# The two score products of a pair of batches put directly behind the attends of the pair before, in the steady step lists of a graph attention kernel

## The chip, the cores and the metric

The kernel runs on one core of one Trainium2 chip. Its time is the device time of one execution in microseconds (us). A run with a profile gives besides that a record of every instruction. Below, PE is TensorE's matmuls and PEld its weight loads, DVE is VectorE, ACT is ScalarE, POOL is GpSimd and SP is SyncE, whose only work here is to issue DMAs.

## The reference

There are 128 batches of 128 nodes with 512 features, and one 128 x 128 adjacency matrix for each batch. Two layers follow one another, each with a residual and a layer norm; all of it is float32.

```python
x: (128, 128, 512) f32;  adj: (128, 128, 128) int32

# layer 0: attention with 8 heads of 64 features
q, k, v = (x @ W + b for W, b in ((Wq, bq), (Wk, bk), (Wv, bv)))
logits = einsum('bqhd,bkhd->bhqk', q, k) / sqrt(64)
attn = softmax(where(adj > 0, logits, -1e9), axis=-1)
out = relu(einsum('bhqk,bkhd->bqhd', attn, v) @ Wo + bo)
x = layernorm(x + out)

# layer 1: one head with additive scores
Wh = x @ W
e = leaky(s_i + s_j)           # s: Wh times the two halves of the vector a
att = softmax(where(adj > 0, e, -1e9), over one node axis)
x = layernorm(x + leaky(att @ Wh))
```

## The kernel before

**Products.** The large products are done by schemes of seven half-size products in place of eight (the names p1 to p7). The products with Wq, Wk and Wv run over groups of four batches (`GROUP`), in six chains a group: Q, K and V, each in two rounds (`group_product`, L658, matmul L681). Their results go to three PSUM banks (`ps_st`, tiles st_y, st_w, st_x) and are taken out by ScalarE copies (L694) and VectorE additions (L715); six, four, three, four, three and four additions a chain then combine them (`combine`, L731). The weights beyond those that stay in SBUF come in through a ring of four buffers w_n (`fetch_until`, L623). The products with Wo and with layer 1's W run over pairs of batches (`pair_product`, L793, matmul L801), in the classes `LayerZero` (z) and `LayerOne` (w).

**Softmax.** `Softmax` (L855) is layer 0's attention of one batch. Its methods are, in order: `scores` (L868; sixteen matmuls L875 on 64-row tiles, two PSUM banks lg), `add` of the mask (L889, twice), `reduce` (maxima, L898), `exp` (ScalarE, L909, eight heads), `reciprocals` (L919), `divide` (ScalarE, L923), `store` of the probabilities to DRAM (L930), `fetch` of them in another layout (L936, four DMAs into the single buffer paz), `transpose` (VectorE, L942), `attend` (sixteen matmuls L955 on 64-column tiles, one bank p_oT) and `copy` (four on ScalarE, L970). The trip through DRAM and back does one half of turning the probabilities, the VectorE transpose of 32 x 32 blocks the other.

**Layer 1.** `Edge` (L1157) is the attention of layer 1 for one batch: `turn_blocks` (L1187), `add` (L1191), `maxima` (L1197), `exp` (L1201), `divide` (L1205 and L1206), `product` (L1211, bank p_h), `copy` (ScalarE, L1218, into the single `z_slot`), `residual` (L1221), `stats` (L1003 and L1005), `rstd` (GpSimd, L1009 and L1011), `apply` (L1024) and `store` (out_dram). `Senders` (v) writes and fetches the node scores ez (L1262).

**PSUM.** `psum` (L201) gives out five banks in turn to p_h, p_oT, lg and the pair products; the group products have their own three.

**Order.** The schedule is written by hand (`tc.manual_schedule`, L1276): every engine executes its instructions in the order in which the Python code issues them. The steady loop (L1541) makes one step for each batch t from 6 to 123, 118 steps, and issues the tokens of the list `STEADY[t % 4]` (L72 to L114) one after the other. In an even step, f is the softmax of batch t and s that of batch t + 1, and both go on through the odd step behind it, at whose end they attend. The letters are:

- f and s the softmaxes; w and z the pair products of layer 1 and 0; e the layer 1 attention, n the end of the batch before's; v the senders; g and p the end of layer 0 (sums, norm, stores, transposes of x1); m the loads, turns and masks of batches to come (x_pair and x_one load x through SP, sum sums x on GpSimd);
- `h` half of the next group product's step on TensorE;
- `a` and `d` the next copy (ACT) or addition (DVE) left over from these;
- `k` and `k.v` the next combination (L731) on GpSimd or VectorE;
- `i.s1a` and the like a part of the inner sums of x (L500) on GpSimd, with `.v` on VectorE;
- `q` the next fetches of weights w_n, through SP.

Of the kernel before, what the change touches and what calls it, by code (L numbers as in the profile page):

```python
# [70 lines left out]

STEADY = {  # L72
    0: """
        k.v n.residual q f.scores h h m.masks m.sum.0 m.sum.1 m.sum.2 m.sum.3 k.v g.apply.0
        q k.v w.p1 f.add.0 f.add.1 g.store.0 e.turn_blocks a e.add m.cast w.t0 s.scores
        f.reduce w.p6 f.exp.0.1 f.exp.2.3 d w.t2 f.exp.4.5 f.exp.6.7 d n.stats s.add.0
        f.reciprocals.0 s.add.1 e.maxima f.reciprocals.1 s.reduce w.p5 h n.rstd w.p7 w.p2 h
        h m.residuals q g.fetch_both a w.t3 e.exp q q w.c22 w.c11 f.divide.2.3 s.exp.2
        f.divide.0.1 a f.divide.6.7 e.divide w.p4 w.p3 h h h w.c21 s.exp.5 v.senders
        f.divide.4.5 s.exp.0.1 a i.s1a.v n.apply d s.exp.6.7 s.exp.3.4 q n.store v.store  # L80
        f.store g.transpose.1 g.transpose.0 i.s3a.v e.product h m.x_pair i.s2a i.s1b m.turn
        d k.v m.mask i.s3b.v a s.reciprocals.0 s.reciprocals.1 w.c12 d i.s2b.v k.v e.copy
        v.fetch
    """,
    1: """
        p.sum.0 z.by n.residual h z.p2 h k h a s.divide.5.6 i.s4a a f.fetch z.p1 h h d
        n.stats n.rstd k.v m.turn e.turn_blocks s.divide.3.4 s.divide.7 s.divide.0.1
        s.divide.2 n.apply z.bw z.t0 h z.p6 z.t2 a m.cast z.p5 z.p7 k k k h z.c11
        f.transpose z.t3 e.add d z.p4 s.store z.c22 a z.p3 h h m.mask e.maxima z.c21 s.fetch
        n.store q e.exp a a d z.stats.1 e.divide i.s4b h e.product h f.attend z.c12 e.copy  # L90
        f.copy p.sum.1 z.rstd.1 p.sum.2 z.apply.1 s.transpose q z.stats.0 d s.attend s.copy
        p.sum.3 z.rstd.0 k k s.sum.2 s.sum.0 s.sum.1 k s.sum.3 m.x_one z.store.1
    """,
    2: """
        f.scores n.residual g.apply.0 w.p1 f.add.1 f.add.0 s.scores e.turn_blocks w.t0 e.add
        w.p6 f.reduce w.t2 w.p2 h w.p7 m.turn k.v k.v f.exp.4.5 f.exp.6.7 f.exp.0.1 k.v w.p5
        h w.t3 a f.exp.2.3 n.stats f.reciprocals.1 w.c22 e.maxima w.c11 f.reciprocals.0
        e.exp f.divide.2.3 n.rstd w.p4 h w.c21 v.senders a d n.apply f.divide.4.5
        f.divide.6.7 f.divide.0.1 e.divide s.add.0 s.add.1 d h w.p3 q g.store.0 m.residuals
        m.masks h e.product h h a a g.fetch_both m.x_one n.store v.store s.reduce  # L100
        g.transpose.0 w.c12 q f.store v.fetch q m.cast d g.transpose.1 m.mask s.exp.5 e.copy
    """,
    3: """
        s.exp.3.4 z.by s.exp.6.7 k.v n.residual n.stats p.sum.0 h f.fetch a s.exp.2 z.p2
        z.p1 h h s.exp.0.1 z.t0 n.rstd q k.v z.p6 p.sum.1 p.sum.2 s.reciprocals.0
        s.reciprocals.1 d s.divide.5.6 a s.divide.0.1 s.divide.7 s.divide.3.4 h
        e.turn_blocks n.apply d z.t2 s.divide.2 m.cast m.turn h a a h z.p7 h h d m.mask
        z.c11 z.bw e.add a z.t3 k k k e.maxima f.transpose k z.p5 q e.exp h h z.p4 h a a d
        z.c22 s.store q q e.divide z.c21 s.fetch z.p3 h d z.stats.1 z.c12 k h n.store
        e.product z.rstd.1 p.sum.3 z.apply.1 d z.stats.0 h h f.attend s.transpose a e.copy a  # L110
        s.attend f.copy s.copy k z.rstd.0 s.sum.0 q z.store.1 s.sum.2 s.sum.1 m.x_one
        s.sum.3
    """,
}  # L114

# [1607 lines left out]
```

## Time and profile before

| | |
|---|---|
| median of 3 runs | 2329.5 us (2326.45 to 2329.78) |
| the profiled execution | 2328.13 us, span from first to last instruction 2325.5 us |
| granted TensorE clock | 0.993 of full |
| DMA, mean over the span | 233 GB/s |
| HBM read and written | 388.96 and 148.31 MB |

Of the groups of instructions those that the lists move most are these: line, engine, operation, tiles written and read, count, then busy time in us and mean ns of one, then idle time of the engine just before them and what ended it.

```profile
L875 PE MATMUL lg<-out_K,out_Q 64*128 64x128 f32 x2048 | 148.7, 285 | 0.8 <-DVE out_K L731 0.8
L955 PE MATMUL p_oT<-pa,out_V 128*64 128x128 f32 x2000 | 136.7, 279 | 18.7 <-DVE pa L942 18.7
L942 DVE STREAM_TRANSPOSE pa<-paz 128x1024 f32<-128x1024 f32 x125 | 154.6, 1237 | 9.6 <-DMA paz<-pa_dram 7.7
L1009 POOL TENSOR_SCALAR ve<-mv 128x1 f32<-128x1 f32 x256 | 77.9, 304 | 288.6 <-DVE mv L1005 226.3
```

The matmuls of one engine overlap, so a mean of 285 ns is the time from start to modelled end of one, not the distance of two. The forms 64*128 and 128*64 after MATMUL are the part of the array that is used: rows by columns.

### The profile page before, as it was taken

How to read it: one execution, taken by the hardware profiler on the slowest of the kernel's cores; microseconds unless marked ns; L12 is line 12 of the kernel's file. 1: busy time of each engine (PE TensorE's matmuls, PEld its weight loads, DVE VectorE, ACT ScalarE, POOL GpSimd, SP SyncE). 2: the span in 40 equal slices, each digit the busy share in tenths (PEclk: the TensorE clock that was granted, in tenths of full speed). 3: DMA queues.
4: the chain of work that ended last, by engine and by line, in shares of the span. 5: the costliest groups of instructions: out<-in, count | busy, mean ns of one | idle time of the engine just before them, and what ended most of it. 6: DMA issues, size and time to landing. Idle time of an engine off the chain costs nothing.

```text
span 2325.5 us, 53031 instructions
## 1 busy us (share of the span) xinstructions
PE 2264.5 (97%) x17394; PEld 2028.0 (87%) x17394; DVE 2116.6 (91%) x4248; ACT 1665.8 (72%) x5971; POOL 1465.7 (63%) x1735
## 2 busy tenths in 40 slices
PE   5999999999999999999999999999999999999998
PEld 5888988888988888889889889889888889888885
DVE  7998999999999999999999999999999999999977
ACT  1766776777777867767767767767767777777686
POOL 4466666667666666666676666676656666666656
PEclk7999999999999999999999999999999999999999
DMA  6978888888888888878888888888888888888774
GB/s 160 269 209 234 238 249 233 233 232 243 242 241 238 230 236 243 242 240 236 225 246 233 250 238 231 233 240 236 247 238 232 234 244 236 243 238 227 221 217 145
DMA packets 516595, 540.81 MB, mean 233 GB/s; under 512 B 100568, under 2 KB 394336, under 8 KB 516320
## 3 DMA queue, kind: packets, MB, share of 16 engines
q1 hardware_dynamic: 516000, 537.17, 80.8%
q8 instruction: 138, 2.26, 0.4%
q14 instruction: 137, 1.12, 0.2%
q10 hardware_dynamic: 320, 0.26, 0.0%
HBM read 388.96 MB, written 148.31 MB: 231 GB/s over the span
## 4 chain that ended last, share of the span: by engine, by line
PE 58%; DVE 19%; DMA 8%; POOL 5%; SPq 4%; issue 3%; ACT 3%; DVEq 0%; POOLq 0%; ACTq 0%
PE p_y L801 14%; PE st_y L681 14%; PE p_w L801 6%; PE lg L875 6%; PE st_w L681 6%; PE st_x L681 5%; DMA w_n<-wv 4%; DVE pa L942 4%; PE p_x L801 4%; PE p_oT L955 3%; DVE arena L1047 2%; DVE cells L715 2%; PE p_h L1211 2%; DVE st L1003 2%; DMA paz<-pa_dram 2%
## 5 line engine op out<-in xcount | busy, mean ns | idle before, releaser
L909 ACT ACTIVATE pa<-pa,nmax 128x128 f32<-128x128 f32 x1000 | 391.7, 398 | 1.9 <-DVE nmax L898 1.8
L923 ACT ACTIVATE pa<-pa,rs 128x128 f32<-128x128 f32 x1000 | 329.0, 398 | 15.4 <-DVE rs L919 15.2
L1009 POOL TENSOR_SCALAR ve<-mv 128x1 f32<-128x1 f32 x256 | 77.9, 304 | 288.6 <-DVE mv L1005 226.3
L694 ACT COPY cells<-st_y 128x384 f32<-128x384 f32 x288 | 136.2, 473 | 115.8 <-PE st_y L681 102.9
L1024 DVE TENSOR_SCALAR arena<-arena,mv,rstd 128x512 f32<-128x512 f32 x239 | 185.5, 776 | 14.3 <-POOL rstd L1011 14.3
L909 ACT ACTIVATION_READ_ACCUMULATOR pa<-pa,nmax 128x1 f32 x1000 | 194.9, 195 | 0.0
L970 ACT ACTIVATE arena<-p_oT,b_cols 128x128 f32<-128x128 f32 x504 | 144.2, 370 | 64.5 <-PE p_oT L955 60.5
L523 POOL TENSOR_TENSOR x1S<-x1T 128x256 f32<-128x256 f32 x62 | 57.6, 928 | 208.2 <-DVE mf L853 208.2
L1011 POOL TENSOR_TENSOR rstd<-ve,mhalf 128x1 f32<-128x1 f32 x256 | 160.6, 627 | 21.4
L1003 DVE BATCH_NORM_STATS2 st<-arena 128x6 f32<-128x512 f32 x248 | 168.0, 677 | 1.1
L942 DVE STREAM_TRANSPOSE pa<-paz 128x1024 f32<-128x1024 f32 x125 | 154.6, 1237 | 9.6 <-DMA paz<-pa_dram 7.7
L889 DVE TENSOR_TENSOR pa<-lg,mf 128x512 f32<-128x512 f32 x250 | 161.2, 675 | 0.9 <-PE lg L875 0.9
L955 PE MATMUL p_oT<-pa,out_V 128*64 128x128 f32 x2000 | 136.7, 279 | 18.7 <-DVE pa L942 18.7
L694 ACT COPY out_V<-st_y 128x512 f32<-128x512 f32 x128 | 74.5, 582 | 109.5 <-PE st_y L681 109.0
L875 PEld LDWEIGHTS lg<-out_K,out_Q 64*128 64x128 f32 x2048 | 124.2, 187 | 31.9 <-issue 20.4
L875 PE MATMUL lg<-out_K,out_Q 64*128 64x128 f32 x2048 | 148.7, 285 | 0.8 <-DVE out_K L731 0.8
L898 DVE TENSOR_REDUCE nmax<-pa 128x8 f32<-128x1024 f32 x125 | 148.4, 1187 | 0.1
L955 PEld LDWEIGHTS p_oT<-pa,out_V 128*64 128x64 f32 x2000 | 106.7, 136 | 42.0 <-DVE pa L942 33.7
L801 PE MATMUL p_y<-wo_w,x1S 128*128 128x257 f32 x496 | 134.3, 393 | 0.1
L1218 ACT ACTIVATE arena<-p_h 128x512 f32<-128x512 f32 x120 | 71.5, 596 | 87.1 <-DMA out_dram<-arena 59.3
L715 DVE TENSOR_TENSOR cells<-st_w,cells 128x384 f32<-128x384 f32 (+1 forms) x224 | 126.7, 566 | 6.5 <-PE st_w L681 2.9
L801 PE MATMUL p_y<-wo_w,x1T 128*128 128x257 f32 x496 | 131.6, 387 | 0.4 <-ACT arena L812 0.4
(296 smaller groups left out, 7960.2 us busy)
## 6 DMA issues: line engine op xcount, KB each, us to landing
paz<-pa_dram SPq DMA_DIRECT2D x504, 128.0 KB, 3.5
pa_dram<-pa SPq DMA_DIRECT2D x125, 512.0 KB, 3.8
w_n<-wk SPq DMA_DIRECT2D x93, 512.0 KB, 5.9
w_n<-wv SPq DMA_DIRECT2D x93, 512.0 KB, 5.0
w_n<-wk SPq DMA_DIRECT2D x93, 384.0 KB, 4.3
w_n<-wv SPq DMA_DIRECT2D x93, 384.0 KB, 5.6
x_dram<-arena SPq DMA_DIRECT2D x128, 256.0 KB, 2.8
xz<-x_dram SPq DMA_DIRECT2D x240, 128.0 KB, 4.2
```

What stands on the lines that cost most here:

```text
L681: nc.tensor.matmul(p[:, index, :], lhs, rhs, start=start and index == 0, stop=True, skip_group_check=True,)
L694: nc.scalar.copy(dst, p)
L715: nc.vector.tensor_add(cells(c)(h, o), p, t)
L801: nc.tensor.matmul(p[:, :width], xs()[n][:, kc, :], w[:, PLACE[n], kc, :], start=start and kc == 0, stop=True, skip_group_check=True,)
L875: nc.tensor.matmul(self.lg[r][:, c, :], q[rows, 2 * (b % 2) + c % 2, c // 2, :], k[rows, 2 * (b % 2) + c % 2, c // 2, :], start=c == 0, st ...
L889: nc.vector.tensor_add(by_head[:, r * NC : (r + 1) * NC], self.lg[r].rearrange("p c (b k) -> p c b k", b=4), mf.unsqueeze(1).to_broadcast( ...
L909: nc.scalar.activation(self.pa[:, :, h, :], self.pa[:, :, h, :], AF.Exp, bias=self.nmax[:, h : h + 1], accum_out=self.sums[:, h : h + 1],)
L923: nc.scalar.activation(self.pa[:, :, h, :], self.pa[:, :, h, :], AF.Copy, scale=self.rs[:, h : h + 1])
L942: nc.vector.transpose(self.paT.rearrange("p h (a i) -> p a h i", i=32), self.paz.rearrange("p a (h k) -> p a h k", k=32),)
L955: nc.tensor.matmul(self.oT[r * HD : (r + 1) * HD, c, :], v[:, c % 2, c // 2, r * HD : (r + 1) * HD], self.paT[:, r * NC + c, :], start=c == 0,
L1003: nc.vector.bn_stats(st, self.src)
L1024: nc.vector.tensor_scalar(self.src, self.src, self.mv[:, 0:1], self.r, ALU.subtract, ALU.mult)
```

## The change

Only the four step lists are changed; no method and no buffer is. Each list is rearranged:

- `s.scores` stands next to `f.scores` in steps 0 and 2, ahead of `w.p1`. Steps 1 and 3 end with `f.attend` and `s.attend` as before, so TensorE has two attends and two score products in a row.
- `f.fetch` goes from step 1 to the end of step 0.
- Of the inner sums, s1b, s3a, s2a and s4b are on VectorE, in place of s1a, s3a, s3b and s2b. In step 0, `i.s1a` on GpSimd stands ahead of `n.rstd`.
- One combination of a group goes from VectorE (`k.v`) to GpSimd (`k`).
- The group product has 9, 11, 9 and 13 half steps (`h`) in the four steps, where it had 9, 11, 7 and 15. Two heads of `s.exp`, one `k.v` and one `d` go from step 3 to step 2.
- In step 1 `z.apply.1` and `m.mask` stand behind `s.transpose`, in place of ahead of it.

```diff
--- before.py
+++ after.py
@@ -71,45 +71,45 @@
 
 STEADY = {
     0: """
-        k.v n.residual q f.scores h h m.masks m.sum.0 m.sum.1 m.sum.2 m.sum.3 k.v g.apply.0
-        q k.v w.p1 f.add.0 f.add.1 g.store.0 e.turn_blocks a e.add m.cast w.t0 s.scores
-        f.reduce w.p6 f.exp.0.1 f.exp.2.3 d w.t2 f.exp.4.5 f.exp.6.7 d n.stats s.add.0
-        f.reciprocals.0 s.add.1 e.maxima f.reciprocals.1 s.reduce w.p5 h n.rstd w.p7 w.p2 h
-        h m.residuals q g.fetch_both a w.t3 e.exp q q w.c22 w.c11 f.divide.2.3 s.exp.2
-        f.divide.0.1 a f.divide.6.7 e.divide w.p4 w.p3 h h h w.c21 s.exp.5 v.senders
-        f.divide.4.5 s.exp.0.1 a i.s1a.v n.apply d s.exp.6.7 s.exp.3.4 q n.store v.store
-        f.store g.transpose.1 g.transpose.0 i.s3a.v e.product h m.x_pair i.s2a i.s1b m.turn
-        d k.v m.mask i.s3b.v a s.reciprocals.0 s.reciprocals.1 w.c12 d i.s2b.v k.v e.copy
-        v.fetch
+        e.turn_blocks f.scores q m.masks q n.residual k.v g.apply.0 g.store.0 q m.residuals
+        q g.fetch_both q q f.add.0 f.add.1 f.reduce s.scores w.p1 m.sum.0 m.sum.2 m.sum.1
+        e.add m.cast w.t0 h w.p6 h h w.p2 f.exp.2.3 f.exp.4.5 w.t2 f.exp.6.7 a s.add.0
+        m.sum.3 e.maxima d s.add.1 d f.reciprocals.1 n.stats f.exp.0.1 a f.divide.4.5
+        f.reciprocals.0 w.p7 i.s1a h h w.c11 s.reduce d w.p5 w.t3 e.exp f.divide.2.3
+        f.divide.6.7 a f.divide.0.1 s.exp.5 e.divide w.c22 w.p4 h w.p3 n.rstd h n.apply
+        w.c21 v.senders s.exp.2 s.exp.3.4 i.s1b.v i.s3a.v a n.store h g.transpose.1
+        g.transpose.0 e.product s.exp.6.7 s.exp.0.1 v.store f.store h m.x_pair v.fetch
+        f.fetch a e.copy d w.c12 k.v m.mask i.s2b i.s3b i.s2a.v s.reciprocals.0 m.turn
+        s.reciprocals.1 d k
     """,
     1: """
-        p.sum.0 z.by n.residual h z.p2 h k h a s.divide.5.6 i.s4a a f.fetch z.p1 h h d
-        n.stats n.rstd k.v m.turn e.turn_blocks s.divide.3.4 s.divide.7 s.divide.0.1
-        s.divide.2 n.apply z.bw z.t0 h z.p6 z.t2 a m.cast z.p5 z.p7 k k k h z.c11
-        f.transpose z.t3 e.add d z.p4 s.store z.c22 a z.p3 h h m.mask e.maxima z.c21 s.fetch
-        n.store q e.exp a a d z.stats.1 e.divide i.s4b h e.product h f.attend z.c12 e.copy
-        f.copy p.sum.1 z.rstd.1 p.sum.2 z.apply.1 s.transpose q z.stats.0 d s.attend s.copy
-        p.sum.3 z.rstd.0 k k s.sum.2 s.sum.0 s.sum.1 k s.sum.3 m.x_one z.store.1
+        z.p2 n.residual i.s4b.v k.v z.by h h s.divide.7 s.divide.5.6 a a i.s4a s.divide.3.4
+        s.divide.0.1 s.divide.2 z.bw h z.p1 h h z.p5 d n.stats k.v k.v z.t0 z.p6 z.t2 a h
+        z.c11 m.turn e.turn_blocks z.p7 h e.add z.t3 z.p4 f.transpose d n.rstd k p.sum.0 k
+        e.maxima z.c22 s.store a h h q z.p3 s.fetch d n.apply z.c21 a m.cast e.exp a
+        e.divide h h e.product m.x_one n.store q f.attend z.stats.1 p.sum.2 z.rstd.1 p.sum.1
+        z.c12 s.transpose s.attend f.copy z.stats.0 m.mask p.sum.3 e.copy s.copy z.rstd.0
+        s.sum.0 d z.apply.1 s.sum.2 s.sum.1 s.sum.3 k k k z.store.1
     """,
     2: """
-        f.scores n.residual g.apply.0 w.p1 f.add.1 f.add.0 s.scores e.turn_blocks w.t0 e.add
-        w.p6 f.reduce w.t2 w.p2 h w.p7 m.turn k.v k.v f.exp.4.5 f.exp.6.7 f.exp.0.1 k.v w.p5
-        h w.t3 a f.exp.2.3 n.stats f.reciprocals.1 w.c22 e.maxima w.c11 f.reciprocals.0
-        e.exp f.divide.2.3 n.rstd w.p4 h w.c21 v.senders a d n.apply f.divide.4.5
-        f.divide.6.7 f.divide.0.1 e.divide s.add.0 s.add.1 d h w.p3 q g.store.0 m.residuals
-        m.masks h e.product h h a a g.fetch_both m.x_one n.store v.store s.reduce
-        g.transpose.0 w.c12 q f.store v.fetch q m.cast d g.transpose.1 m.mask s.exp.5 e.copy
+        f.scores g.apply.0 q m.masks s.scores w.p1 f.add.0 f.add.1 w.t0 f.reduce h h w.p6
+        f.exp.4.5 f.exp.2.3 w.p2 w.t2 w.p7 e.turn_blocks g.store.0 n.residual s.add.0 k.v
+        k.v k.v f.exp.6.7 e.add w.p5 a s.add.1 m.turn f.reciprocals.1 e.maxima n.stats w.t3
+        f.exp.0.1 f.divide.4.5 h w.p4 a e.exp d h h w.c21 m.cast f.reciprocals.0 w.c11
+        v.senders m.residuals n.rstd n.apply d f.divide.2.3 a a f.divide.6.7 f.divide.0.1 h
+        e.divide m.mask e.product s.reduce d w.c22 k.v h h g.fetch_both m.x_one w.p3 n.store
+        v.store q h f.store q s.exp.6.7 g.transpose.0 v.fetch e.copy s.exp.5 d g.transpose.1
+        w.c12
     """,
     3: """
-        s.exp.3.4 z.by s.exp.6.7 k.v n.residual n.stats p.sum.0 h f.fetch a s.exp.2 z.p2
-        z.p1 h h s.exp.0.1 z.t0 n.rstd q k.v z.p6 p.sum.1 p.sum.2 s.reciprocals.0
-        s.reciprocals.1 d s.divide.5.6 a s.divide.0.1 s.divide.7 s.divide.3.4 h
-        e.turn_blocks n.apply d z.t2 s.divide.2 m.cast m.turn h a a h z.p7 h h d m.mask
-        z.c11 z.bw e.add a z.t3 k k k e.maxima f.transpose k z.p5 q e.exp h h z.p4 h a a d
-        z.c22 s.store q q e.divide z.c21 s.fetch z.p3 h d z.stats.1 z.c12 k h n.store
-        e.product z.rstd.1 p.sum.3 z.apply.1 d z.stats.0 h h f.attend s.transpose a e.copy a
-        s.attend f.copy s.copy k z.rstd.0 s.sum.0 q z.store.1 s.sum.2 s.sum.1 m.x_one
-        s.sum.3
+        a s.exp.3.4 z.by h z.p1 s.exp.0.1 s.exp.2 k k a z.t0 s.reciprocals.1 s.reciprocals.0
+        n.residual d k z.p2 n.stats p.sum.0 h s.divide.5.6 s.divide.3.4 s.divide.2 m.turn
+        e.turn_blocks z.p6 h h m.cast s.divide.7 s.divide.0.1 z.t2 e.add z.bw a a p.sum.1
+        n.rstd p.sum.2 z.p7 z.p5 h h q m.x_one f.fetch z.t3 a q s.store d m.mask n.apply
+        z.c11 e.maxima k p.sum.3 k k z.c22 f.transpose q q z.p4 h h z.p3 h e.exp a z.c21 d
+        z.stats.1 d s.fetch h h z.c12 e.divide n.store e.product a a h h z.rstd.1 z.apply.1
+        d k k k.v z.stats.0 e.copy s.transpose f.attend z.rstd.0 s.attend a f.copy s.copy
+        s.sum.2 s.sum.0 s.sum.1 s.sum.3 z.store.1 q
     """,
 }
```

## The prediction

> **What bounds the kernel now.** I read the page first, then one window over the steady loop, the waits in it, and the TensorE and VectorE timelines of one group of four steps. The page:
>
> ```profile
> span 2325.5 us, 53031 instructions
> PE 2264.5 (97%) x17394; PEld 2028.0 (87%) x17394; DVE 2116.6 (91%) x4248; ACT 1665.8 (72%) x5971; POOL 1465.7 (63%) x1735
> ```
>
> TensorE is busy 97% of the span, VectorE 91%. The window 300 to 2150 us leaves the opening and the ending out:
>
> ```profile
> core 0: us, PE busy (x) PEld busy (x) DVE busy (x) ACT busy (x) POOL busy (x), PEclk, DMA share, GB/s
> 300.00:2150.00 1850.00, 1838.48 (x14222) 1653.20 (x14220) 1706.08 (x3445) 1358.27 (x4901) 1180.12 (x1391) 1.00 0.83 238
> ```
>
> TensorE's gaps are 11.5 us of 1850, at full clock: it is the bound, and only TensorE's time can be won. In the timeline the same product recurs every 70.42 us (1035.17 is followed by its like one group later), so a group of four steps costs 70.42. Per group VectorE has 1706.08 x 70.42 / 1850 = 64.9 us of work, so 5.5 us free. It is nearly a second bound. The waits of the window (engine, line, what for: us in total, times, longest):
>
> ```profile
> ACT arena L1218 <- DMA out_dram<-arena: 52.3, 26, 3.0
> PEld p_oT L955 <- DVE pa L942: 24.1, 52, 0.5
> PEld lg L875 <- issue: 17.6, 78, 0.3
> PE p_oT L955 <- DVE pa L942: 11.5, 52, 0.2
> ```
>
> 52 waits in 26 groups: at every pair of batches the second attend waits for VectorE's transpose L942. Busy TensorE also hides something, seen in start times (start, duration, instruction):
>
> ```profile
> 1035.17 1.09 PE L955 MATMUL p_oT<-pa,out_V 128*64 128x128 f32 x16
> 1036.46 1.09 PE L955 MATMUL p_oT<-pa,out_V 128*64 128x128 f32 x16 [0.20 <-DVE pa L942]
> 1037.49 1.16 PE L875 MATMUL lg<-out_K,out_Q 64*128 64x128 f32 x16
> 1038.58 0.49 PE L681 MATMUL st_x<-w_n,xT 128*128 128x128 f32 x2
> ...
> 1040.47 1.03 PE L801 MATMUL p_y<-wo_w,x1T 128*128 128x257 f32 x4
> 1041.43 1.16 PE L875 MATMUL lg<-out_K,out_Q 64*128 64x128 f32 x16
> 1042.53 1.14 PE L801 MATMUL p_y<-wo_w,x1S 128*128 128x257 f32 x4
> 1043.50 1.03 PE L801 MATMUL p_w<-wo_w,x1S 128*128 128x257 f32 x4
> 1044.37 0.38 PE L681 MATMUL st_y<-w_n,xT 128*128 128x128 f32 x2
> ```
>
> A p_w product of four, 1043.50 to the next start, takes 0.87. The p_y ahead of the lone scores (64-row tiles, L875) takes 0.96 (1040.47 to 1041.43), and the one behind them 0.97 (1042.53 to 1043.50). The 16 scores take 1.10 instead of 0.90, by the records' 112 ns between starts of small matmuls. Thus an island of half-array products between full-array ones costs 0.09 + 0.20 + 0.10 = 0.39 us. Attend, attend and the first scores stand together already, so per pair there are two groups of half-array products: that run and the lone s.scores.
>
> **What the Trainium skill says.** "TensorEngine Tiling (Array Packing)", Key Properties: "Changing tiling mode (not just tile) drains the TensorE". The trace agrees as far as the 0.39 goes; the direct step from attends (128x64 tiles) to scores (64x128) is in both kernels once per pair, so it doesn't enter. "TensorE: Matmul & The Clock Gate", the architectural detail on sub-arrays: VectorE and ScalarE queues are strictly first in, first out, TensorE pulls only weight loads ahead; so a list order is binding, and a late VectorE operation delays all behind it. "SBUF — State Buffer", Who interferes with whom: VectorE operations with a two-port mode and GpSimd share one port pair, exclusively. The trace agrees: L1024 takes 0.54 alone and 0.95 beside GpSimd work:
>
> ```profile
> 1048.99 0.54 DVE L1024 TENSOR_SCALAR arena<-arena,mv,rstd 128x512 f32<-128x512 f32 x1
> 1062.44 1.25 DVE L942 STREAM_TRANSPOSE pa<-paz 128x1024 f32<-128x1024 f32 x1 [0.73 <-DMA paz<-pa_dram]
> 1069.02 0.95 DVE L1024 TENSOR_SCALAR arena<-arena,mv,rstd 128x512 f32<-128x512 f32 x1
> 1069.89 1.23 DVE L942 STREAM_TRANSPOSE pa<-paz 128x1024 f32<-128x1024 f32 x1
> ```
>
> **The change part by part**, per group of four steps, two pairs of batches.
>
> 1. s.scores moves up to f.scores (steps 0 and 2). The sixteen matmuls stay; the two switches of mode around them go: 2 x 0.39 = 0.79 us less of TensorE itself.
>
> 2. The wait at the second attend. Its transpose (L942) ends at 1071.12 and the attend starts at 1071.18; in the single records its first matmul starts 0.465 to 0.523 behind the first attend's last, where matmuls of one run stand 0.10 apart, and takes 0.05 more itself: 0.41 to 0.47 a pair, I take 0.44, 0.88 a group. In the new list of step 1 the mask and z.apply.1 (L1024, 0.95) stand behind s.transpose instead of ahead (n.apply comes in between); of step 3, a correction (L715) and a combination (L731) go to step 2; and one combination (k.v, 0.65 us) a group goes to GpSimd. So this wait goes, if VectorE is on time otherwise; a wait of 0.08 a group before p_h (L1211) goes too. Gain 0.96.
>
> 3. GpSimd gets that combination: 1.27 us by the row of L731 on POOL. It has 1180 of 1850 us of work, so it costs nothing by itself, but i.s1a (1.4) and the combination now stand ahead of n.rstd in step 0, so L1024 of that step starts at about 12.2 us after the attends' end instead of 11.6, and the transposes of x1 (L426) end at 15.0 to 15.5 instead of 14.4. SP issues only behind these: x_pair's store and loads, v.fetch, then the four f.fetch loads (paz), which landed 8.4 to 10.7 after. f.fetch moves from step 1's list to step 0's end, but on SP it follows v.fetch in both; it is moved past nothing. f.transpose thus comes at 24.3 to 26.2. It is followed by 7.85 us of VectorE work to the end of s.transpose, so 32.2 to 34.1; TensorE, with nothing to wait for, would reach the second attend at 32.8 to 33.0. New wait 0 to 1.1; I take 0.25, the early half, as the transpose waited only 0.03 to 0.73 before.
>
> 4. Step 2: the first product of the group product's third chain (chain 2, bank st) has to wait until the d token of chain 1 (L715) has emptied its bank, and on VectorE that stands behind two adds (1.2), reduce (1.1), e_turned (0.22), n.residual (0.6), the second softmax's two adds (1.2), three combinations (1.63), m.turn (0.62), reciprocal and maxima (0.35), stats (0.8) and its own 0.46: 8.1 us from the first add, which starts 1.5 to 2.3 after the attends. TensorE gets there at 9.27. Wait 0.1 to 1.2; I take 0.5. Queued behind it on TensorE are all products of the step; VectorE's later work is not held up by it, save by what TensorE's late results feed.
>
> 5. Five PSUM banks serve p_h, two attends and three products in turn; joined, the run p_h, attend, attend, scores, scores (two banks each) needs more than five, so the last scores reuse the banks of p_h and of the first attend, and w.p1 that of the second. They wait for e.copy (L1218) and f.copy (L970). "PSUM — Partial Sum Buffer", PSUM: the matmul accumulator, gives 8 banks in all; the kernel has 5 here and 3 for st, so no free one. e.copy itself waits for the out_dram store (52.3 us in 26 groups, up to 3.0), which on SP in step 1 now stands behind s.fetch's four issues and m.x_one's four (about 0.45 each). Worked out from the issues: e.copy ends about 7.4 after f.transpose, the scores are due at 8.45. Cost nothing, with 1 us cover; if the cover is gone, each us late is one us of TensorE.
>
> 6. The rest: `h`, `q`, `a` in other places. A weight fetch has still 6.2 us from free buffer to use (7.0 before), so nothing. The last product of chain 0 waits 0 to 0.35 for a ScalarE copy behind the divides. 0.2 for all of it.
>
> Sum per group: -0.79 - 0.96 + 0.25 + 0.50 + 0.20 = -0.80. The loop has 118 steps, 29.5 groups: -23.6 us. The profiled run took 2328.1, span 2325.5 and 2.6 around it: 2304.5. The median of the runs is 1.4 higher: 2305.9. I say 2305.
>
> **The rivals.**
> - No new wait: 2 and 1 come in full, and VectorE's 5.5 us idle absorb 3 and 4. For: VectorE loses 0.65 us of work a group. Against: its order in step 2 is tight. -1.75 x 29.5 = -52: 2278. Chance 0.12.
> - VectorE gives it all back: a wait of s.transpose's kind elsewhere, at f.transpose or at chain 2's product, of 1.75 us in sum (upper ends of 3, 4 and 6: 2.65). For: idle of 5.5 us at 70.42 and VectorE's stalls for paz and for stats on GpSimd are in order. 2325 to 2333. Chance 0.09.
> - Slower: the bank chain of part 5. The place is the last scores, behind e.copy, behind the out_dram store, behind SP. Up to 1.05 us lateness it costs nothing; 2.1 us late at both pairs costs 2 x 1.05, -1.75 + 2.1 = +0.35 a group, 2339. It decides from about 2 us late; L1218 already waits 2 us a group on average (52.3 / 26), which speaks for it; the cover of 1 us, after which the wait only begins, speaks against. Chance 0.13.
> - That the change doesn't do what it says: the list makes the run contiguous, and a stall within it changes no mode, so 0.79 stays. I give this no chance of its own.
>
> **How the numbers follow.** Partial gain (2284 to 2324) 0.66, as above for the others. Measurements here tell 0.2%, 4.7 us, from no change: below 2324.8 is faster, above 2334.2 slower. Faster 0.66 + 0.12 + 0.01 = 0.79, same 0.08, slower 0.13. All new waits at their lower ends: -1.65 x 29.5, 2281; for the upper end I take the given-back case's middle, 2331, as all three waits at upper ends together (2355) contradict the idle VectorE has. Left out: half of the first rival, the slower one.
>
> **What would show it.** Group period about 69.6; no L942 wait at the second attend of step 3; products before and after scores at 0.87 and one pitch; st_y or st_x at step 2 waiting for DVE about 0.5; a small wait at L942 in step 1. I am wrong if lg waits for ACT L1218, if the period stays at 70.4, or if both attend waits remain.

## The result and the profile after

The changed kernel takes 2357.07 us in the median of 4 runs (2354.56 to 2358.25), the kernel before 2329.34 beside it: ratio 1.012, 95% interval 1.0103 to 1.0138. It is slower by 27.7 us, where 24 us less were forecast. The profiled execution spans 2355.2 us. The page of the changed kernel, span and busy time:

```profile
span 2355.2 us, 53157 instructions
PE 2275.6 (97%) x17394; PEld 2027.4 (86%) x17394; DVE 2110.6 (90%) x4217; ACT 1654.4 (70%) x5971; POOL 1538.5 (65%) x1766
```

A group of four steps takes 71.36 us in place of 70.42, by the starts of the attends. The difference of 0.94 us times 29.5 groups is the 27.7 us, so the whole loss lies in the steady loop. The joined run is there as planned. TensorE's timeline at the end of a step 1 (start, duration, instruction):

```profile
1079.87 1.97 PE L955 MATMUL p_oT<-pa,out_V 128*64 128x128 f32 x32
1081.77 2.08 PE L875 MATMUL lg<-out_K,out_Q 64*128 64x128 f32 x32
1083.78 1.14 PE L801 MATMUL p_y<-wo_w,x1T 128*128 128x257 f32 x4
```

No product stands between, no wait is marked. What TensorE waits for now, in the same window of 300 to 2150 us as before (us in total, times, longest):

```profile
PEld st_y L681 <- ACT cells L694: 26.1, 49, 0.8
...
PEld st_y L681 <- DVE cells L715: 19.2, 26, 0.7
...
PEld p_y L801 <- ACT pr_t L812: 10.3, 26, 0.4
...
PEld st_y L681 <- ACT cells L700: 8.3, 26, 0.3
PEld st_y L681 <- DVE out_Q L715: 7.3, 26, 0.3
...
PEld p_oT L955 <- DVE pa L942: 1.4, 3, 0.8
```

The 52 waits at the attends that the prediction shows are down to 3 (last line). In their place stand waits for ScalarE copies and VectorE additions that empty the banks of the group product. To get sizes, the start times of all matmuls of 24 groups were laid over the token lists, and each product's time taken from its start to the next one's. Per group of four steps, in us:

| term of the sum | predicted | measured |
|---|---|---|
| switches of mode around the lone scores | -0.79 | -0.77 |
| waits at the second attends and at p_h | -0.96 | -0.80 |
| step 1: before z.p4 0.51, around chain 1's p1 0.49 | +0.25 | +1.00 |
| step 2: before chain 2's p1 | +0.50 | +0.61 |
| rest: step 0 before chain 5's p1 0.25, step 2 before chain 1's p7 0.65 | +0.20 | +0.90 |
| sum | -0.80 | +0.94 |

Both gains came. Two of the three prices were some four times too small. Where do they come from? In step 2, the wait before chain 1's p7 followed back through TensorE, ScalarE, VectorE and GpSimd:

```profile
1090.14 0.49 PE L681 MATMUL st_y<-xS,wq 128*128 128x128 f32 x2 [0.41 <-ACT cells L694]
...
1089.61 0.48 ACT L694 COPY cells<-st_y 128x384 f32<-128x384 f32 x1 [1.01 <-DVE out_Q L731]
...
1086.84 1.81 DVE L731 TENSOR_TENSOR out_Q<-cells 128x256 f32<-128x256 f32 x2
1088.58 0.94 DVE L731 TENSOR_TENSOR out_Q<-cells,out_Q 128x256 f32<-128x256 f32 x1
...
1086.78 2.46 POOL L731 TENSOR_TENSOR out_Q<-out_Q 128x256 f32<-128x256 f32 x3
```

The copy writes the buffer `cells` that VectorE's three combinations read, so it waits for their end. They take 1086.84 to 1089.52, while GpSimd does three of its own from 1086.78. In the kernel before, GpSimd did two of them before the sums of s.sum and one among them. Behind this, on the same two engines, comes the wait before chain 2's p1. The first line is the first add of the mask (f.add), the second the addition that has to empty the bank:

```profile
1082.96 1.29 DVE L889 TENSOR_TENSOR pa<-lg,mf 128x512 f32<-128x512 f32 x2
...
1091.71 0.53 DVE L715 TENSOR_TENSOR cells<-st_x,cells_t 128x384 f32<-128x384 f32 x1
...
1092.29 0.49 PE L681 MATMUL st_y<-xT,w_n 128*128 128x128 f32 x2 [0.34 <-DVE cells L715]
```

In step 1 VectorE and GpSimd meet in the same way with the inner sums:

```profile
1066.07 1.66 DVE L500 TENSOR_TENSOR inner_s<-xS,inner_s 128x384 f32<-128x384 f32 x1 [0.59 <-PE st_w L681]
...
1066.05 1.27 POOL L500 TENSOR_TENSOR inner_s<-xT,inner_s 128x512 f32<-128x512 f32 x1 [1.12 <-PE st_w L681]
...
1072.71 0.40 ACT L1191 ACTIVATE att<-e_turned,arena 128x128 f32<-128x128 f32 x1 [0.94 <-DVE e_turned L1187]
1073.02 0.35 ACT L812 COPY pr_t<-p_y 128x256 f32<-128x256 f32 x1
...
1073.42 1.13 PE L801 MATMUL p_y<-wo_w,arena 128*128 128x256 f32 x4 [0.21 <-ACT pr_t L812]
```

s4b on VectorE and s4a on GpSimd wait for the same product of TensorE (st_w), so they start together, and s4b takes 1.66 us. VectorE is then late with e_turned, ScalarE waits with e.add, and the copy z.t3 that stands behind it is what z.p4 waits for. VectorE has a combination less per group, 0.65 us, but its busy time in one group is not smaller. Rows of the windows view, before and after (window, length, busy us of PE, PEld, DVE, ACT, POOL with counts, clock, DMA share, GB/s):

```profile
1035.17:1105.59 70.42, 69.98 (x543) 62.94 (x543) 64.50 (x132) 51.68 (x187) 45.09 (x54) 1.00 0.81 240
```

```profile
1044.70:1116.10 71.40, 70.28 (x545) 62.79 (x544) 64.93 (x131) 51.47 (x187) 47.67 (x55) 1.00 0.80 236
```

This sum alone doesn't show the fault, because other instructions became shorter. The normalizations of L1024, eight in a group, before and after (count, busy us, mean ns, idle before):

```profile
L1024 DVE TENSOR_SCALAR arena<-arena,mv,rstd 128x512 f32<-128x512 f32 x210 | 162.7, 775 | 11.9 <-POOL rstd L1011 11.9
```

```profile
L1024 DVE TENSOR_SCALAR arena<-arena,mv,rstd 128x512 f32<-128x512 f32 x206 | 122.0, 592 | 20.8 <-POOL rstd L1011 16.0
```

They win 8 x 0.18 = 1.5 us a group. So VectorE loses only about 1 us a group in sum (0.43, and the 0.65 of the combination that it no longer does). What costs is the place: at the two new slow stretches TensorE waits for what comes behind.

### The profile page after: what moved, and what is told of

Same layout as the page of the kernel before. It is cut to its first block, busy times and chain, and to the rows that moved or that the text cites. A ratio compares the mean times of both kernels' runs of the same rounds, so it can differ in the third digit from the quotient of the medians.

```text
span 2355.2 us, 53157 instructions
## 1 busy us (share of the span) xinstructions
PE 2275.6 (97%) x17394; PEld 2027.4 (86%) x17394; DVE 2110.6 (90%) x4217; ACT 1654.4 (70%) x5971; POOL 1538.5 (65%) x1766
## 4 chain that ended last, share of the span: by engine, by line
PE 59%; DVE 18%; DMA 7%; SPq 5%; ACT 4%; issue 3%; POOL 3%; DVEq 0%; POOLq 0%; ACTq 0%
PE st_y L681 17%; PE p_y L801 10%; PE st_w L681 9%; PE p_w L801 6%; PE p_oT L955 5%; PE lg L875 4%; PE p_h L1211 4%; PE st_x L681 3%; DVE pa L889 3%; DMA paz<-pa_dram 3%; DVE out_Q L731 3%; PE p_x L801 3%; DVE xT L426 2%; DMA xz<-x_dram 2%; SPq L421 2%
## 5 line engine op out<-in xcount | busy, mean ns | idle before, releaser
L731 POOL TENSOR_TENSOR out_Q<-out_Q,cells 128x512 f32<-128x512 f32 x92 | 116.1, 1276 | 137.8 <-DVE out_Q L731 127.9
L1011 POOL TENSOR_TENSOR rstd<-ve,mhalf 128x1 f32<-128x1 f32 x256 | 187.0, 730 | 21.3
L1024 DVE TENSOR_SCALAR arena<-arena,mv,rstd 128x512 f32<-128x512 f32 x239 | 141.9, 594 | 23.3 <-POOL rstd L1011 17.8
L731 POOL TENSOR_TENSOR out_K<-out_K 128x512 f32<-128x512 f32 x91 | 121.9, 1353 | 34.3 <-PE p_y L801 29.0
L731 POOL TENSOR_TENSOR out_K<-out_K,cells 128x512 f32<-128x512 f32 x63 | 95.6, 1519 | 68.9 <-DVE cells L715 64.4
L801 PE MATMUL p_y<-wo_w,arena 128*128 128x256 f32 x504 | 132.6, 386 | 5.8 <-ACT pr_t L812 5.8
L875 PE MATMUL lg<-out_K,out_Q 64*128 64x128 f32 x2048 | 134.6, 280 | 0.8 <-DVE out_K L731 0.8
L955 PE MATMUL p_oT<-pa,out_V 128*64 128x128 f32 x2000 | 127.9, 279 | 6.6 <-DVE pa L942 6.6
```

Of the source, the lines that this page charges most:

```text
L731: (by or engine).tensor_add(*(t(n) for t, n in (dst, left, right)))
L801: nc.tensor.matmul(p[:, :width], xs()[n][:, kc, :], w[:, PLACE[n], kc, :], start=start and kc == 0, stop=True, skip_group_check=True,)
L875: nc.tensor.matmul(self.lg[r][:, c, :], q[rows, 2 * (b % 2) + c % 2, c // 2, :], k[rows, 2 * (b % 2) + c % 2, c // 2, :], start=c == 0, st ...
L955: nc.tensor.matmul(self.oT[r * HD : (r + 1) * HD, c, :], v[:, c % 2, c // 2, r * HD : (r + 1) * HD], self.paT[:, r * NC + c, :], start=c == 0,
L1011: nc.gpsimd.tensor_tensor(self.r, ve, mhalf, ALU.pow)
```

## The experiments

Theory A: the joined run is good, and the loss comes from VectorE and GpSimd working side by side at two new places. Its rivals are that the joined run itself brings the waits (B), or that VectorE as a whole sets the pace, so that a stall only moves (C). All times are medians, each with the ratio to the kernel before, run on the same chip. The kernel before took 2326.4 to 2327.1 us beside these runs and 2329.3 beside the changed kernel; differences from the changed kernel are therefore given by the medians and, where it matters, by the ratios too.

**join: the run alone in the old lists.**

```diff
 # step 0
-f.scores h h
+f.scores s.scores h h
...
-w.t0 s.scores
+w.t0
 # step 2
-f.scores n.residual
+f.scores s.scores n.residual
...
-f.add.0 s.scores
+f.add.0
```

> The kernel before with s.scores directly behind f.scores in steps 0 and 2, and nothing else moved. Theory A (the joined run is worth its two switches of mode, 0.77 us a group in the trace of the changed kernel, and the loss comes from the other moves): 29.5 x 0.77 = 23 us less, 2307; not below 2300. Theory B (the joined run itself brings the loss, since the second scores come before VectorE and the banks are ready for what follows): 2335 or more.

2423.14 us, ratio 1.0418 (1.0402 to 1.0433). In this kernel the second scores of step 0 read K ahead of its last combinations, so its values are others. A missed by far. The place where step 0 loses most, on VectorE, ScalarE and TensorE:

```profile
1079.11 0.73 DVE L731 TENSOR_TENSOR out_K<-out_K,cells 128x512 f32<-128x512 f32 x1 [1.78 <-PE lg L875]
...
1083.21 0.40 ACT L1191 ACTIVATE att<-e_turned,arena 128x128 f32<-128x128 f32 x1 [1.32 <-DVE e_turned L1187]
...
1083.70 0.37 ACT L812 COPY arena<-p_y 128x257 f32<-128x257 f32 x1
...
1081.10 1.03 PE L801 MATMUL p_y<-wo_w,x1T 128*128 128x257 f32 x4
1084.12 1.14 PE L801 MATMUL p_y<-wo_w,x1S 128*128 128x257 f32 x4 [1.99 <-ACT arena L812]
```

The two products are w.p1 and w.p6. The scores had stood between them, and their 1.1 us covered the copy w.t0 (L812) that w.p6 waits for. In step 2 w.p6 waits for this copy too, with 0.55 us in the profile's bracket. B is right in this: a run that is joined takes a filler away, and something must stand in its place. But the 96 us are not the price of the joined run alone. In step 0 a combination of K waits 1.78 us for the second scores, which read K in this order; e_turned stands behind it on VectorE, e.add (L1191) waits for e_turned, and w.t0 stands behind e.add on ScalarE. And in 15 of the 25 groups between 300 and 2150 us the trace shows TensorE at half its clock for 3.4 us behind this wait, in one of them here (the number ahead of the last two is the clock):

```profile
1158.00:1161.00 3.00, 3.00 (x11) 2.64 (x11) 2.89 (x9) 2.50 (x13) 2.82 (x4) 0.50 1.17 229
```

The kernel before has no such stretch in this window. A group with one takes some 74.3 us, a group without 72.7; 1.6 us in 15 of 25 groups are, by an estimate from these numbers, 28 of the 96 us.

**join2: the run with fillers.**

```diff
 # step 0
-k.v n.residual q f.scores h h
+k.v k.v k.v q f.scores s.scores w.p1 n.residual h h
...
-f.add.1 g.store.0 e.turn_blocks a e.add m.cast w.t0 s.scores
+f.add.1 w.t0 g.store.0 e.turn_blocks a e.add m.cast
... (two k.v that now stand ahead of the scores, and w.p1, leave their old places)
 # step 2
-f.scores n.residual g.apply.0 w.p1 f.add.1 f.add.0 s.scores e.turn_blocks w.t0
+f.scores s.scores n.residual g.apply.0 w.p1 f.add.1 f.add.0 w.t0 h e.turn_blocks
...
-w.p2 h w.p7
+w.p2 w.p7
```

> The kernel before with the joined run alone, and with what it needs: in step 0 the last three combinations of chain 3 ahead of the scores, in both even steps w.t0 earlier on ScalarE and half steps of the group product between w.p1 and w.p6, where the scores stood. Theory A: 0.77 x 29.5 = 23 us less than the kernel before, 2304, if VectorE's three combinations are not late. Theory B (the join can't be had without new waits of that size): 2325 or more.

2350.54 us, ratio 1.0099 (1.0084 to 1.0114): B's number. The waits at the attends stayed, and new ones for ScalarE copies came:

```profile
PEld p_y L801 <- ACT arena L812: 19.5, 26, 0.8
...
PEld st_y L681 <- ACT cells L694: 15.2, 26, 0.6
```

So in the old lists the join costs more than it brings, in the two arrangements tried. That the changed lists suffer from it too isn't said by that.

**nojoin: the changed kernel without the run.**

```diff
 # steps 0 and 2
-s.scores w.p1
+w.p1 s.scores
```

> The changed kernel with s.scores back behind w.p1 in both even steps. Theory A: the two switches come back, 0.77 us a group, but behind them TensorE waits for others 1.5 us a group anyway, and that takes some of it: 2357 to 2380. Theory B: faster than the changed kernel by 10 us or more, below 2347.

2358.74 us, ratio 1.0139 (1.0123 to 1.0156). This is 2 us more than the changed kernel, 4 by the ratios. B falls for the changed lists: without the run they are as slow. Little of the run's gain is seen either. The wait before chain 1's p7 shrank from 0.65 to 0.30 us, and that of 0.25 before chain 5's p1 is gone, since TensorE came later: what the run saves ahead of a late VectorE, TensorE waits for behind it.

**s4b and s4b_later: the collision in step 1.** First the sum goes back to GpSimd, then it stays on VectorE but at another time.

```diff
 # s4b, step 1
-n.residual i.s4b.v k.v
+n.residual k.v
...
-a a i.s4a s.divide.3.4
+a a i.s4a i.s4b s.divide.3.4
```

> The changed kernel with the inner sum s4b of step 1 on GpSimd again, behind s4a, as it was before the change. Theory A (VectorE is late in step 1 because s4b waits 0.5 us for TensorE and then takes 1.66 in place of 0.55 us beside GpSimd's s4a; TensorE then waits 0.96 us a group for a ScalarE copy and for a VectorE addition): 29.5 x 0.96 = 28 us less, 2329 or better. Theory B: within 6 us of the changed kernel, since the stalls would come back behind the next scores.

2324.32 us, ratio 0.9991 (0.9982 to 1.0000). This is 33 us less than the changed kernel, 30 by the ratios: A's number, and B falls. The waits before z.p4 and around chain 1's p1 are gone, those of step 2 unchanged.

```diff
 # s4b_later, step 1
-n.residual i.s4b.v k.v
+n.residual k.v
...
-d n.stats k.v k.v
+d n.stats i.s4b.v k.v k.v
```

> The changed kernel with the inner sum s4b still on VectorE, but behind n.stats of step 1, when GpSimd has finished s4a and waits. Theory A (it is the collision and the wait for TensorE that cost, 1.66 + 0.54 us, not the sum's own work): s4b takes 0.55 us, VectorE wins 1.65 us, and most of TensorE's 1.0 us a group in step 1 goes: 20 to 29 us less than the changed kernel, 2328 to 2337. Theory F (any s4b on VectorE in step 1 is too much work there): less than 10 us gained, above 2347.

2324.46 us, ratio 0.9992 (0.9983 to 1.0001): 33 us less than the changed kernel, 30 by the ratios, a little more than A said. The row of this sum on VectorE, first in the changed kernel, then here (count, busy us, mean ns, idle before):

```profile
L500 DVE TENSOR_TENSOR inner_s<-xS,inner_s 128x384 f32<-128x384 f32 x26 | 43.2, 1661 | 13.9 <-PE st_w L681 13.9
```

```profile
L500 DVE TENSOR_TENSOR inner_s<-xS,inner_s 128x384 f32<-128x384 f32 x26 | 13.6, 525 | 0.0
```

The same instruction on the same engine, started 1.4 us later (22.8 us after the start of the attends in place of 21.4): 525 ns in place of 1661, and no wait. F falls.

**kpool: the collision in step 2.**

```diff
 # step 1
-z.rstd.0 s.sum.0 d z.apply.1 s.sum.2 s.sum.1 s.sum.3 k k k
+z.rstd.0 d z.apply.1 k k s.sum.0 s.sum.2 s.sum.1 k s.sum.3
```

> The changed kernel with GpSimd's three combinations at the end of step 1 in the places of the kernel before: two ahead of the sums of s.sum, one among them. Theory A (VectorE's three combinations in step 2 take 2.75 in place of 1.79 us because GpSimd's three run beside them; the ScalarE copy of chain 1 waits for the last of them, and TensorE for the copy): TensorE's wait of 0.65 us a group before chain 1's p7 goes, and part of the 0.6 us before chain 2's p1: 19 to 30 us less, 2327 to 2338. Theory B: within 6 us of the changed kernel.

2332.16 us, ratio 1.0024 (1.0014 to 1.0034), 25 us less than the changed kernel, 22 by the ratios: A's number. VectorE's combinations in the changed kernel and here:

```profile
L731 DVE TENSOR_TENSOR out_Q<-cells 128x256 f32<-128x256 f32 x52 | 46.6, 934 | 0.0
...
L731 DVE TENSOR_TENSOR out_Q<-cells,out_Q 128x256 f32<-128x256 f32 x26 | 24.5, 942 | 0.0
```

```profile
L731 DVE TENSOR_TENSOR out_Q<-cells 128x256 f32<-128x256 f32 x54 | 20.1, 410 | 0.0
...
L731 DVE TENSOR_TENSOR out_Q<-cells,out_Q 128x256 f32<-128x256 f32 x27 | 11.1, 412 | 0.0
```

Nothing of VectorE's list was moved, only GpSimd's, and each combination takes 0.41 in place of 0.94 us (in a group 1.2 against 2.8). In exchange n.residual of this step (L1221), which now stands beside GpSimd's additions, takes 1.20 us in place of 0.67, so that VectorE wins about 1 us of the 1.6. The wait before chain 1's p7 is gone, that before chain 2's p1 is 0.29 in place of 0.61.

**fix2: both repairs.** The two edits s4b and kpool together.

> The changed kernel with both repairs at once: s4b on GpSimd, and GpSimd's combinations at the end of step 1 ahead of and among the sums. Theory A (two separate collisions of VectorE with GpSimd): the gains add, 2324 + 2332 - 2357 = 2299, between 2294 and 2306. Theory C (VectorE as a whole is the bound, and a stall that is removed in one step comes back in another): 2318 or more.

2299.66 us, ratio 0.9881 (0.9866 to 0.9895). The gains add to within 1 us by the medians and 3 us by the ratios, the group takes 69.43 us, and C falls.

**fix3 and fix4: two additions earlier.**

```diff
 # step 0
-a s.add.0 m.sum.3 e.maxima d s.add.1
+a d s.add.0 m.sum.3 e.maxima s.add.1
 # step 2
-s.add.1 m.turn
+s.add.1 d m.turn
...
-e.exp d h h
+e.exp h h
```

> As fix2, and two additions of the group product (L715) earlier on VectorE: in step 2 that of chain 1 ahead of m.turn, the maxima and the stats, in step 0 that of chain 4 ahead of s.add.0. Theory A: TensorE's waits of 0.29 us before chain 2's p1 and 0.23 before chain 5's p1 go, 0.52 x 29.5 = 15 us less than fix2, near 2284. Theory C: within 5 us of fix2 or slower.

2309.85 us, ratio 0.9923 (0.9907 to 0.9940): 10 us more than fix2: A missed, and the number is C's. The wait before chain 2's p1 is gone and that of step 0 smaller, but a new one stands in step 2 (VectorE, then TensorE):

```profile
1073.87 0.55 DVE L1024 TENSOR_SCALAR arena<-arena,mv,rstd 128x512 f32<-128x512 f32 x1 [0.61 <-POOL rstd L1011]
...
1074.94 0.49 PE L681 MATMUL st_w<-xT,wq 128*128 128x128 f32 x2 [0.50 <-DVE cells L715]
```

The addition had filled the time between the stats and rstd. Without it VectorE waits 0.61 us for GpSimd, and the next addition, queued behind, is late. fix4 puts that one into the hole:

```diff
 # step 2
-n.rstd n.apply d
+n.rstd d n.apply
```

> As fix3, and in step 2 the addition of chain 1's c22 (L715) ahead of n.apply on VectorE, in the 0.61 us in which VectorE waits there for rstd. Theory A (fix3 lost only because the first addition, moved away from between the stats and n.apply, left that hole, and the next addition came late for TensorE by 0.77 us a group): 23 us less than fix3, 2287, between 2280 and 2294. Theory C (VectorE as a whole sets the pace in step 2): another wait comes, 2300 or more.

2295.31 us, ratio 0.9861 (0.9843 to 0.9878): 14.5 us less than fix3, the lowest time of all runs. It lies between A's range and C's. The wait of step 2 went with the hole, so the hole was its cause, but a part of the gain is missing: waits of 0.20 us a group before chain 2's p5 and 0.16 before chain 5's p5 remain.

**fix3_nojoin and fix4_nojoin: what the run is worth where less is late.** The edit of nojoin on both.

> As fix3, with s.scores back behind w.p1 in both even steps. Theory A (the joined run is worth 0.77 us a group wherever nothing behind it is late): 23 us more than fix3, near 2307. Theory D (the run is worth little, because what stands behind it sets the pace as in nojoin, where it made 2 us): within 7 us of fix3.

2314.40 us, 4.6 more than fix3.

> As fix4, with s.scores back behind w.p1 in both even steps. Theory A: where no wait is left behind the scores, the joined run is worth its whole 0.77 us a group: 23 us more than fix4. Theory D (it is worth a few us only): within 7 us of fix4.

2301.53 us, ratio 0.9889 (0.9873 to 0.9904), 6.2 more than fix4. D's numbers, not A's: TensorE spends 0.77 us less in the run, but in fix4 some 0.36 us a group of small waits stand behind it that fix4_nojoin doesn't have. Whether there are lists in which the whole 0.77 reaches the end wasn't tried.

**attend: the transpose earlier, in the old lists.**

```diff
 # step 1
-z.apply.1 s.transpose q
+s.transpose z.apply.1 q
 # step 3
-z.stats.0 h h f.attend s.transpose
+h h f.attend s.transpose z.stats.0
```

> The kernel before, with s.transpose ahead of z.apply.1 in step 1 and ahead of z.stats.0 in step 3 on VectorE, nothing else. Theory A (the waits at the second attend can be had without the joined run): 0.88 x 29.5 = 26 us less than the kernel before, 2301, between 2297 and 2312. Theory E (what stands behind the transpose is as urgent, and the wait comes back): within 5 us of the kernel before.

2308.68 us, ratio 0.9916 (0.9898 to 0.9934). This lies in A's range, and E falls. The profiled execution is the fastest of the four (2302.66 to 2311.51): most of its groups take 69.53 us, 0.89 less than before, which is A's number, a few 70.57, and why these few are longer stays open. Two tokens moved in the old lists bring two thirds of what fix2 does.

## Why the prediction was wrong

- **The bound.** Right: the loop is paced by TensorE and each wait of it counts in full.
- **Part 1, the switches of mode.** Right: 0.77 for 0.79. That this is a gain of the whole kernel was not: nojoin, fix3_nojoin and fix4_nojoin show 2 to 6 us of the 23, since it is won ahead of waits.
- **Part 2, the waits at the attends.** Right in kind, 0.80 for 0.96, and attend shows that it needs no joined run.
- **Part 3, step 1.** This term failed. I followed n.apply, the DMAs and f.transpose, where no wait came, and asked of the moved inner sums only what i.s1a delays on GpSimd. s4b, moved to VectorE, starts with GpSimd's s4a and took 1.66 us; I hadn't priced it. The 0.25, meant for another wait, was 1.00, and s4b and s4b_later take all of it away.
- **Part 4, chain 2's p1.** Right in place, 0.61 for 0.50, but in size partly by luck. The sum behind it took 1.63 us for three combinations that took 2.6 to 2.8, and from the first add to the end of the addition VectorE needed 9.3 us (1082.96 to 1092.24) where I had 8.1. Against that it began 1.1 us after the attends, earlier than my 1.5 to 2.3, and TensorE came 0.65 us later, because it had just waited for the copy. Half of the wait went with kpool.
- **Part 5, the banks.** Right: no scores wait for L1218, and the rival that ends on the slow side, which was this chain, didn't occur. The loss came from the mechanism of the second rival, VectorE late, at a size (2.5 us of new waits) that I had inside the sum of the upper ends and left out of the range, because VectorE's idle time seemed to exclude it. That 2.5 comes near the 2.65 of the upper ends is chance, since the waits of parts 3 and 6 were others than those that I had summed. (The middle of the second rival's case, 2325 to 2333, is 2329 and not the 2331 that I took for the upper end.)
- **Part 6, the rest.** Failed: 0.90 for 0.20. The copy that waits for `cells` (0.65) wasn't in my list of waits, and kpool shows the collision as its cause. For the 0.25 us before chain 5's p1 no run isolates a cause; in fix3 an earlier addition takes it away.

The common fault: I quoted the Trainium skill ("SBUF — State Buffer", Who interferes with whom) on the exclusive port pair with L1024's 0.54 and 0.95 us beside it, but only for operations with a two-port mode. The same section names a VectorE instruction with two SBUF inputs beside a GpSimd instruction that reads SBUF as well, and these are what s4b and the combinations are; the trace agrees, with 1.66 and 0.94 us. Nor was the 0.54 taken alone: GpSimd's inner sum began 0.23 us behind that L1024 and took 1.45 us, where GpSimd had already begun in the case with 0.95. The two cases differ in which engine started first. I then used VectorE's old durations for each moved instruction. A row's mean holds for the neighbours that it had.

GpSimd beside these two, first at 1048.99, then at 1069.02, in the kernel before:

```profile
1049.22 1.45 POOL L500 TENSOR_TENSOR inner_s<-inner_s,xT 128x512 f32<-128x512 f32 x1 [1.38 <-DVE inner_s L500]
```

```profile
1068.60 1.09 POOL L525 TENSOR_TENSOR x1S<-x1T 128x256 f32<-128x256 f32 x1
```

## What to carry to other kernels

When a list moves work of VectorE or GpSimd, lay the two queues over each other in time, and price work with two SBUF operands at its duration beside the other engine wherever both wait for the same event. Such a slow stretch costs where TensorE waits for what comes behind it, so look there first. A joined run saves its switches, but it takes a filler away and brings TensorE earlier to what stands behind it; the saving counts only when that is ready. Moving an operation out of the time in which its engine would wait opens a hole: put the next one into it.

## What the runs showed of the hardware

- An addition of two SBUF operands on VectorE beside GpSimd additions takes 0.94 in place of 0.41 us (128x256), and 1.66 in place of 0.53 (128x384): more than twice, three times in the second case. In both places GpSimd starts first, by 0.06 and 0.02 us in the groups shown, and VectorE bears nearly all of it: GpSimd's three take 2.46 us, 0.82 each, against 0.73 for one in kpool, and its s4a takes 1.27 us, as in s4b_later, where s4b comes behind it.
- Where VectorE starts first, GpSimd bears it. The two lines below are of step 1 of the changed kernel, 0.06 us apart: VectorE keeps its 0.69 us, and GpSimd takes 1.76 where additions of this size take 1.27 in the same trace (L731, `out_V<-out_V,cells`). This order holds in all 26 groups between 300 and 2150 us, and the same is seen at a combination of K, where VectorE starts 0.04 us ahead: 0.69 us on VectorE, 1.78 on GpSimd.
- After each wait TensorE's first small product takes some 0.10 us more (starts 0.213 apart in place of 0.112), as after a switch of mode. So a wait costs TensorE more than the bracket of its matmul shows: 0.65 us where it reads 0.41 (chain 1's p7), 0.61 where it reads 0.34 (chain 2's p1).

```profile
1063.11 0.69 DVE L500 TENSOR_TENSOR inner_s<-inner_s,xT 128x512 f32<-128x512 f32 x1
...
1063.17 1.76 POOL L731 TENSOR_TENSOR out_V<-out_V 128x512 f32<-128x512 f32 x1 [0.94 <-DVE out_V L731]
```
